# One block of a linear layer by a level of Strassen's algorithm, and a weight load in two halves

## The chip, the cores and the metric

The kernel runs on one core of one Trainium2 chip. The time is the device time of one execution in microseconds (us). Three runs of the kernel before gave 1405.92 to 1406.15 us, with a median of 1406.15 us. Besides these there is one execution under the hardware profiler. Everything said of single instructions comes from that one.

## The reference

`x` is 1024 x 512, `weight` holds 64 matrices of 512 x 512, and everything is fp32.

```python
out_lin = x @ lin_w.T + lin_b
xv = jnp.einsum('bf,efm->bem', x, weight)
zp = jnp.einsum('bf,efm->bem', jnp.square(x), jnp.square(weight))
interaction = 0.5 * jnp.sum(jnp.square(xv) - zp, axis=1)
return out_lin + interaction
```

There are 64 large products, `x @ weight[e]`, whose squares are summed, one product of squares, and one small product for the linear layer, `x @ lin_w.T`. The change is in the linear layer.

## The kernel before

**The blocks.** `x` is cut into four blocks by rows r and by columns kk: A11 (0, 0), A12 (0, 1), A21 (1, 0) and A22 (1, 1). Each block has four quarters of 256 columns on 128 partitions. In the names of the code, block "1" is A11, "2" is A12 and "4" is A22, and `xs[:, SLOT[i], SLOT[o]]`, reached as `xsl(i, o)`, is quarter or sum o of block or sum i. The host has laid out `x` and `lin_w.T` so that a block's quarters are contiguous.

**Strassen's algorithm in this kernel.** The main loop multiplies with two nested levels of Strassen's algorithm (its Winograd form): seven products instead of eight, in return for sums of the operands and of the results. `outer_x` makes the sums "5", "6", "7" and "3" of whole blocks (L154 to L176), `inner_x` the four sums of quarters within one block (L178 to L185), and `outer_t` and `inner_t` the sums of the weights. One product of the inner level is called "1", "5", "6", "2", "7", "3" or "4", and these are made in this order. They go to three PSUM banks x, v and y: "1" and "2" to x, "5" and "3" to v, and "6", "7" and "4" to y, which starts as a copy of x after "1". Between two products into the same bank another engine has to read that bank, so TensorE waits for that engine before the second.

**The linear layer before.** It comes ahead of the main loop, while the first weights are being loaded. `lin_w.T` has four row groups k, loaded in `load_lw` (L135), 0 and 1 by ScalarE's queue and 2 and 3 together by SyncE's.

- Rows r = 0: `lin(kk)` (L204 to L222) multiplies A11 (kk = 0) and A12 (kk = 1) directly: eight matmuls of 128x512 each. `lin_out` (L224) then writes twice the sum to `acc[0]` with ScalarE.
- Rows r = 1: `lin_p` (L260) multiplies A21 and A22 by one level of Strassen's algorithm, four matmuls of 128x256 for each of the seven products. `twice` (ScalarE) and `lin_join` (L307, VectorE) write the results to `acc[1]`. The operands' sums are made by `lin_t` (L282, GpSimd) from `lin_w.T`, and by `a21_a22_sums` (L240) from `x`, on VectorE except for the last, which GpSimd makes.

**What sets the order.** There is no scheduler. `Stream` (L14) sorts the pieces by a number t that is written by hand (`st.at(t, fn)`), and every engine gets its instructions in that order. Each engine works through its own in order, and waits at an instruction whose semaphores are not there yet. The pieces around the change are those with t below 0: `lin` at -30 and -22, `lin_out` from -20 to -14, the products of r = 1 from -14 to -2, two steps apart, and the sums of `x` in the table at L587: `inner_x("1")` -29, `inner_x("2")` -22, `a21_a22_sums` -20, `outer_x("5") + inner_x("5")` -16, and `outer_x("6") + inner_x("6")` -3.4. GpSimd's share of this stage is `lin_t`, one sum of A22 (L252), and then the sums of the first weights (`inner_t`, L384, and `outer_t`, L373). The main loop's units (`unit`, L413) start at t = 0, with the x bank's first product at L421.

The DMA semaphores of the queues that SyncE and ScalarE issue are given out in turn from eight. A DMA waits until the one eight places ahead of it has landed.

Of the kernel before, what the change touches and what calls it, by code (L numbers as in the profile page):

```python
# [8 lines left out]
F32 = mybir.dt.float32  # L9
AF = mybir.ActivationFunctionType  # L10
ALU = mybir.AluOpType
# [17 lines left out]
def kernel(  # L29
# [77 lines left out]
    def xsl(i, o):  # L107
        return xs[:, SLOT[i], SLOT[o], :]

    st = Stream()  # L110
# [5 lines left out]
    lw_sb = T6.rearrange("p u l m -> p (u l) m")  # L116
    lw_src = lin_wT.rearrange("(p k) m -> p k m", k=NK)
# [7 lines left out]
    def load_x(r, kk, *parts):  # L125
        src = x[:, 2 * r + kk]
        for w in parts:
            if (r, kk) == (1, 0):
                nc.sync.dma_start(A21[:, w], src[:, w])
                continue  # L130
            (i,) = (i for i, rk in BLOCK.items() if rk == (r, kk))
            dst = a21[i] if w == 3 else xs[:, SLOT[i], w]
            nc.sync.dma_start(dst, src[:, w])

    def load_lw(queue, k):  # L135
        queue.dma_start(lw_sb[:, k], lw_src[:, k])

    for k in range(2):
        load_lw(nc.scalar, k)
    load_x(0, 0, 0, 3, slice(1, 3))  # L140
    load_lw(nc.sync, slice(2, 4))
    load_x(0, 1, slice(0, 3), 3)
# [3 lines left out]
    def quarter(r, kk, n):  # L146

        w = slice(0, 3) if n is None else n
        for i, rk in BLOCK.items():
            if rk == (r, kk):  # L150
                return a21[i] if n == 3 else xs[:, SLOT[i], w, :]
        return A21[:, w, :]

    def outer_x(i, eng=nc.vector):  # L154
        if i in BLOCK:
            return []

        def put(n):
            w = slice(0, 3) if n is None else n

            def of(o):
                return a21[o] if n == 3 else xs[:, SLOT[o], w, :]

            def src(r, kk):
                return quarter(r, kk, n)

            if i == "5":
                eng.tensor_add(of(i), src(1, 0), src(1, 1))
            elif i == "6":
                eng.tensor_sub(of(i), of("5"), src(0, 0))  # L170
            elif i == "7":
                eng.tensor_sub(of(i), src(0, 0), src(1, 0))
            else:
                eng.tensor_sub(of(i), src(0, 1), of("6"))

        return [lambda: put(None), lambda: put(3)]  # L176

    def inner_x(i, eng=nc.vector):  # L178
        add, sub = eng.tensor_add, eng.tensor_sub
        return [  # L180
            lambda: add(xsl(i, "5"), a21[i], xsl(i, "4")),
            lambda: sub(xsl(i, "6"), xsl(i, "5"), xsl(i, "1")),
            lambda: sub(xsl(i, "7"), xsl(i, "1"), a21[i]),
            lambda: sub(xsl(i, "3"), xsl(i, "2"), xsl(i, "6")),
        ]  # L185
# [7 lines left out]
    LIN = {}  # L193
# [7 lines left out]
            ps = psum.tile([P, BK], F32, tag="y", name=f"y_spin{n}", bufs=3)  # L201
            nc.tensor.matmul(ps, zero[:, 0:P], zero, start=True, stop=True)

    def lin(kk):  # L204

        order = [(s, j, l) for s in range(2) for j in range(2) for l in range(2)]
        if kk == 0:
            order.sort(key=lambda o: o[2])
        for s, j, l in order:
            n = 2 * s + j  # L210
            if kk == 0 and l == 0:
# [4 lines left out]
            nc.tensor.matmul(  # L216
                LIN[n],
                quarter(0, kk, (0, 1, 3, 2)[2 * s + l])[:, ts(j, P)],
                lw_sb[:, 2 * kk + l, :],
                start=(kk == 0 and l == 0),  # L220
                stop=(kk == 1 and l == 1),
            )  # L222
# [10 lines left out]
    def lin_x(kk, o):  # L233
# [6 lines left out]
    def a21_a22_sums():  # L240
        def put(kk, o, eng):
            def of(o):
                return lin_x(kk, o)

            raw = a21["4"] if kk else A21[:, 3]
            fn, a, b = {
                "5": lambda: (eng.tensor_add, raw, of("4")),
                "6": lambda: (eng.tensor_sub, of("5"), of("1")),
                "7": lambda: (eng.tensor_sub, of("1"), raw),
                "3": lambda: (eng.tensor_sub, of("2"), of("6")),  # L250
            }[o]()
            fn(of(o), a, b)  # L252

        return [
            lambda o=o, kk=kk: put(kk, o, nc.gpsimd if o == "3" and kk else nc.vector)
            for o in "5673"
            for kk in range(2)
        ]

    def lin_p(o, bank, first):  # L260
        def fn():
            if o == "1":
                for n in "xvy":
                    LIN[n] = psum.tile(
                        [P, BK], F32, tag=n, name=f"{n}_lin", bufs=2 if n == "x" else 3
                    )
                s_lin = spool.tile([P, 2, BK], F32, tag="s", name="s_lin")
                LIN["s2"], LIN["s5"] = s_lin[:, 0], s_lin[:, 1]
            for kk in range(2):
                for j in range(2):  # L270
                    nc.tensor.matmul(  # L271
                        LIN[bank][:, ts(j, HM)],
                        lin_x(kk, o)[:, ts(j, P)],
                        lin_rhs(lw_sb[:, ts(kk, 2)], LT[kk], o),
                        start=(first and kk == 0 and j == 0),
                        stop=True,
                        skip_group_check=True,
                    )

        return fn  # L280
# [13 lines left out]
    def lin_rhs(b, t, o):  # L294
        if o in "123":
            l, u = {"1": (0, 0), "2": (1, 0), "3": (1, 1)}[o]
            return b[:, l, ts(u, HM)]
        return t[:, "5764".index(o)]

    def twice(bank, dst):  # L300
        def fn():
            o = by_j(LIN[dst]) if dst in ("s5", "s2") else acc_blk(1, dst)
            nc.scalar.activation(o, by_j(LIN[bank]), AF.Copy, scale=2.0)

        return fn

    def lin_join(bank, s, blk):  # L307
        def fn():
            nc.vector.scalar_tensor_tensor(
                acc_blk(1, blk),  # L310
                by_j(LIN[bank]),
                2.0,
                by_j(LIN[s]),
                ALU.mult,
                ALU.add,
            )

        return fn

    st.at(-40, spin)  # L320
    for kk in range(2):
        st.at(-30 + 8 * kk, lambda kk=kk: lin(kk))
        st.at(-30 + kk, lambda kk=kk: lin_t(LT[kk], lw_sb[:, ts(kk, 2)]))
    for n in range(4):
        st.at(-20 + 2 * n, lambda n=n: lin_out(n))
    for t, fn in (
        (-14, lin_p("1", "x", True)),
        (-13.5, lambda: nc.scalar.copy(LIN["y"], LIN["x"])),
        (-12, lin_p("5", "v", True)),
        (-11.5, twice("v", "s5")),  # L330
        (-10, lin_p("6", "y", False)),
        (-9.5, twice("y", "s2")),
        (-8, lin_p("2", "x", False)),
        (-7.5, twice("x", 0)),
        (-6, lin_p("7", "y", False)),
        (-5.5, lin_join("y", "s5", 3)),
        (-4, lin_p("3", "v", False)),
        (-3.5, lin_join("v", "s2", 1)),
        (-2, lin_p("4", "y", False)),
        (-1.5, twice("y", 2)),  # L340
    ):
        st.at(t, fn)

    bias = const.tile([P, M], F32, tag="bias", name="bias")

# [189 lines left out]
    for q in range(NQ):  # L535
# [29 lines left out]
        for k, n, r, times in (  # L565
# [5 lines left out]
            for j in range(2):  # L571
                t = g0 + 14 * k + 7 * j + 14.6
# [11 lines left out]
        st.at(-100, lambda kk=kk, v=v: load_w(0, kk, v))  # L584


    for sums, t in (  # L587
        (inner_x("1"), -29),
        (inner_x("2"), -22),
        (a21_a22_sums(), -20),  # L590
        (outer_x("5") + inner_x("5"), -16),
        (outer_x("6") + inner_x("6"), -3.4),
    ):
        for n, fn in enumerate(sums):
            st.at(t + 0.1 * n, fn)
# [236 lines left out]
```

## Time and profile before

| what | value |
|---|---|
| median of three runs | 1406.15 us |
| the profiled execution's own time | 1405.72 us |
| its span, from the first to the last instruction | 1403.9 us |
| TensorE busy | 1399.7 us of the span |
| first matmul of the linear layer | at 4.44 us |
| first matmul of the main loop (L421) | at 30.36 us |

The profile's columns are the start in us from the beginning of the span, the duration, the engine, the line and the instruction with its output and inputs. In brackets stands how long the engine was idle before, and what ended that. A 128x512 fp32 matmul leaves two records and a 128x256 one also two, each half as long. TensorE's instructions overlap, so their cost is read from the distance of the starts, not from the durations.

### The profile page before, as it was taken

Reading aid. Unit: us, or ns where it says so; the run is one execution under the profiler, and the core shown is the slowest. Engines: PE = TensorE matmul, PEld = TensorE weight load, DVE = VectorE, ACT = ScalarE, POOL = GpSimd, SP = SyncE. Lnnn points to the kernel's source line nnn. Section 1 sums busy time; section 2 is a strip of 40 time slices with the busy share of each in tenths; the row PEclk is TensorE's granted clock in tenths of the full one; section 3 lists DMA queues with packets and bytes.
Section 4 is the critical chain, followed back from the end, with each engine's and each line's share of the span. In section 5 each row is a group of like instructions: output and inputs, shape, how many; then the busy total and the mean of one; then the engine's idle time right before and its main releaser. Section 6 shows DMA issues by size and latency. Waiting matters only on the chain.

```text
span 1403.9 us, 11169 instructions
## 1 busy us (share of the span) xinstructions
PE 1399.7 (100%) x3340; PEld 634.8 (45%) x3340; DVE 869.0 (62%) x1263; ACT 620.9 (44%) x825; POOL 1257.8 (90%) x816
## 2 busy tenths in 40 slices
PE   9999999999999999999999999999999999999999
PEld 5444444444444444444444444444444444444446
DVE  6665656656566665656656566565656656566565
ACT  3444353453535444353453535444353453435443
POOL 7989899998999989898998989989898998989984
PEclk9999999999999999999999999999999999999999
DMA  5299898999989989898999989889898999989975
GB/s 217 60 225 213 192 203 175 221 187 218 197 180 225 182 206 210 192 207 174 222 187 217 202 178 224 179 206 209 199 202 175 225 185 217 202 181 221 181 166 135
DMA packets 58108, 273.63 MB, mean 195 GB/s; under 512 B 5440, under 2 KB 8000, under 8 KB 41792
## 3 DMA queue, kind: packets, MB, share of 16 engines
q0 software_dynamic: 36432, 198.20, 72.0%
q1 hardware_dynamic: 21328, 74.19, 15.1%
q10 hardware_dynamic: 288, 0.52, 0.1%
q8 instruction: 27, 0.44, 0.1%
q14 instruction: 33, 0.27, 0.1%
HBM read 72.61 MB, written 2.10 MB: 53 GB/s over the span
## 4 chain that ended last, share of the span: by engine, by line
PE 99%; DMA 0%; DVE 0%; issue 0%
PE y L421 41%; PE v L421 27%; PE x L421 27%; PE lin L216 1%; PE y_last L659 1%; PE x_last L659 0%; PE v_last L659 0%; PE y_lin L271 0%; DMA t<-lin_wT 0%; PE v_lin L271 0%; PE x_lin L271 0%; PE end L722 0%; DVE z L732 0%
## 5 line engine op out<-in xcount | busy, mean ns | idle before, releaser
L421 PE MATMUL y<-t,xs 128*128 128x512 f32 x896 | 421.3, 592 | 0.0
L475 ACT COPY y<-x 128x512 f32<-128x512 f32 x224 | 127.7, 570 | 610.9 <-PE x L421 610.8
L467 DVE TENSOR_TENSOR z<-y,s 128x512 f32<-128x512 f32 x192 | 132.6, 691 | 242.9 <-PE y L421 242.9
L421 PEld LDWEIGHTS y<-t,xs 128*128 128x128 f32 x896 | 170.1, 190 | 214.2 <-issue 210.4
L497 ACT ACTIVATE z<-z 128x1024 f32<-128x1024 f32 x256 | 260.2, 1054 | 12.0 <-POOL z L472 9.4
L421 PE MATMUL x<-w,xs 128*128 128x512 f32 x512 | 248.4, 592 | 0.0
L421 PE MATMUL v<-tp,xs 128*128 128x512 f32 x448 | 228.8, 592 | 0.0
L421 PE MATMUL y<-tp,xs 128*128 128x512 f32 x448 | 228.8, 592 | 0.0
L506 POOL DMA_DIRECT2D acc<-z x190 | 212.9, 1151 | 15.1 <-DMA acc<-z 11.0
L391 POOL TENSOR_TENSOR tp<-w 128x1024 f32<-128x1024 f32 x64 | 174.9, 2734 | 23.8 <-PE y L421 22.6
L421 PE MATMUL x<-t,xs 128*128 128x512 f32 x384 | 188.3, 592 | 0.0
L472 POOL TENSOR_TENSOR z<-z,s 128x1024 f32<-128x1024 f32 x64 | 149.6, 2354 | 42.7 <-DVE s L467 42.7
L467 DVE TENSOR_TENSOR z<-v,s 128x512 f32<-128x512 f32 x192 | 132.6, 691 | 72.5 <-PE v L421 71.0
L458 DVE TENSOR_TENSOR z<-y,z 128x512 f32<-128x512 f32 x192 | 132.3, 689 | 57.9 <-PE y L421 57.9
L380 POOL TENSOR_TENSOR t<-w,t 128x1024 f32<-128x1024 f32 x64 | 164.2, 2728 | 0.0
L458 DVE TENSOR_TENSOR z<-x,z 128x512 f32<-128x512 f32 x192 | 132.1, 688 | 36.6 <-PE x L421 35.1
L421 PEld LDWEIGHTS x<-w,xs 128*128 128x128 f32 x512 | 97.3, 190 | 122.0 <-issue 121.0
L391 POOL TENSOR_TENSOR tp<-t 128x1024 f32<-128x1024 f32 x48 | 130.0, 2708 | 19.2 <-PE y L421 19.1
L421 PEld LDWEIGHTS v<-tp,xs 128*128 128x128 f32 x448 | 85.1, 190 | 107.1 <-issue 103.1
L421 PEld LDWEIGHTS y<-tp,xs 128*128 128x128 f32 x448 | 85.1, 190 | 106.7 <-issue 106.7
L421 PE MATMUL v<-w,xs 128*128 128x512 f32 x256 | 130.7, 592 | 0.0
L446 DVE TENSOR_TENSOR s<-v,z 128x512 f32<-128x512 f32 x160 | 110.5, 691 | 29.4 <-PE v L421 28.7
(114 smaller groups left out, 1475.7 us busy)
## 6 DMA issues: line engine op xcount, KB each, us to landing
w<-weight SPq DMA_DIRECT2D x64, 1024.0 KB, 13.4
acc<-z POOLq DMA_DIRECT2D x128, 512.0 KB, 8.2
w_sum<-w_sb POOLq DMA_DIRECT2D x63, 1024.0 KB, 9.3
acc<-z POOLq DMA_DIRECT2D x62, 1024.0 KB, 8.1
w<-x SPq DMA_DIRECT2D x2, 1024.0 KB, 8.0
out<-z SPq DMA_DIRECT2D x7, 256.0 KB, 2.3
xs<-x SPq DMA_DIRECT2D x2, 384.0 KB, 7.0
t<-lin_wT ACTq DMA_DIRECT2D x2, 256.0 KB, 4.0
```

Of the source, the lines that this page charges most:

```text
L216: nc.tensor.matmul(LIN[n], quarter(0, kk, (0, 1, 3, 2)[2 * s + l])[:, ts(j, P)], lw_sb[:, 2 * kk + l, :], start=(kk == 0 and l == 0), stop ...
L380: nc.gpsimd.tensor_sub(OUTER[i][:, u], a[:, u], b[:, u])
L391: nc.gpsimd.tensor_sub(t, b[:, 1], b[:, :, 0])
L421: nc.tensor.matmul(d[bank], xsl(i, o)[:, ts(j, P)], operand_b(q, i, o), start=start, stop=True, skip_group_check=True,)
L446: nc.vector.tensor_add(o, d[bank], zblk(q, addend, j, b))
L458: nc.vector.tensor_add(zblk(q, dst, j, b), d[bank], zblk(q, addend, j, b))
L467: nc.vector.tensor_add(s if both else zblk(q, dst, j, b), d[bank], s)
L472: nc.gpsimd.tensor_add(place(q, n)[:, 1, j], place(q, src)[:, 1, j], d["s"])
L475: st.at(t0 + 0.5, lambda: nc.scalar.copy(d["y"], d["x"]))
L497: lambda u=u: nc.scalar.activation(z[:, u, j], z[:, u, j], AF.Square),
L506: nc.gpsimd.dma_start(o, z, accum_op=ALU.add)
L659: nc.tensor.matmul(ps[:, ts(j, HM)], last_x(i)[:, (0, 1, 3, 2)[2 * s + l], ts(j, P)], last_w(i)[:, l, :], start=(start and j == 0 and l == 0),
```

## The change

A12's part of the rows r = 0 is no longer multiplied directly. `lin` keeps A11's eight matmuls; the first two of them are cut into two column halves each, in the order (half 0, j 0), (half 0, j 1), (half 1, j 0), (half 1, j 1), and the load of row group 0 of `lin_w.T` is cut in the same halves. `lin_out` writes A11's part to `acc[0]`, and the seven products of A12 follow through `lin_p` with r = 0, two matmuls of 128x256 each, one step of t apart. Their results are added to `acc[0]` by a new `lin_add` on VectorE, which also takes the place of `lin_join` for r = 1:

```diff
-    for k in range(2):
-        load_lw(nc.scalar, k)
+    for u in range(2):
+        load_lw(nc.scalar, 0, ts(u, HM))
+    load_lw(nc.scalar, 1)
...
-    def lin(kk):
-
-        order = [(s, j, l) for s in range(2) for j in range(2) for l in range(2)]
-        if kk == 0:
-            order.sort(key=lambda o: o[2])
+    def lin():
+
+
+        order = [
+            (s, j, l, slice(0, M)) for l in range(2) for s in range(2) for j in range(2)
+        ]
+        order[0:2] = [(0, j, 0, ts(u, HM)) for u in range(2) for j in range(2)]
...
-    def lin_p(o, bank, first):
+    def lin_p(r, o, bank, first):
...
+            kks = range(2) if r else (1,)
+            for kk in kks:
                 for j in range(2):
                     nc.tensor.matmul(
-                        LIN[bank][:, ts(j, HM)],
-                        lin_x(kk, o)[:, ts(j, P)],
+                        LIN[r, bank][:, ts(j, HM)],
+                        lin_x(kk, o, r)[:, ts(j, P)],
                         lin_rhs(lw_sb[:, ts(kk, 2)], LT[kk], o),
...
+    def lin_add(r, bank, addend, dst):
...
+            nc.vector.scalar_tensor_tensor(
+                of(dst), by_j(LIN[r, bank]), 2.0, of(addend), ALU.mult, ALU.add
             )
...
+    for r, t0, dt in ((0, -21.5, 1), (1, -14, 2)):
...
+                ("1", "x", True, copy_y),
+                ("5", "v", True, twice("v", "s5") if r else lin_add(0, "v", 3, "s5")),
+                ("6", "y", False, twice("y", "s2") if r else lin_add(0, "y", 1, "s2")),
+                ("2", "x", False, twice("x", 0) if r else lin_add(0, "x", 0, 0)),
+                ("7", "y", False, lin_add(r, "y", "s5", 3)),
+                ("3", "v", False, lin_add(r, "v", "s2", 1)),
+                ("4", "y", False, twice("y", 2) if r else lin_add(0, "y", 2, 2)),
...
+            st.at(t0 + dt * n, lin_p(r, o, bank, first))
+            st.at(t0 + dt * n + 0.25 * dt, fn)
...
-        (a21_a22_sums(), -20),
-        (outer_x("5") + inner_x("5"), -16),
-        (outer_x("6") + inner_x("6"), -3.4),
+        (a21_a22_sums(), -21, -19.5, -18.5, -16.5, -15.5, -15),
+        (outer_x("5") + outer_x("6"), -14.5),
+        (inner_x("6") + inner_x("5"), -3.4),
```

The last hunk moves VectorE's sums. The sums of A21 and A22 are dealt out between the additions of r = 0. `outer_x("6")` moves ahead of the products of r = 1, beside `outer_x("5")`, and `inner_x("5")` moves behind them.

On VectorE the order of the built kernel, after `inner_x("2")`, is this ("add" is `lin_add` with the product that it follows, z and xs are A21's and A22's sums): z5, add "5", xs5, add "6", z6, add "2", add "7", xs6, add "3", z7, add "4", xs7, z3, the two instructions of `outer_x("5")`, the two of `outer_x("6")`, then for r = 1 add "7" and add "3", then `inner_x("6")` and `inner_x("5")`, and then the main loop. GpSimd's order is unchanged: six instructions of `lin_t`, A22's sum "3", which waits for xs6, and then the weights' sums.

More of the change, by code (lines that the diff above doesn't have):

```diff
@@ L133, in load_x, with load_lw @@
             nc.sync.dma_start(dst, src[:, w])
-    def load_lw(queue, k):
-        queue.dma_start(lw_sb[:, k], lw_src[:, k])
-    for k in range(2):
-        load_lw(nc.scalar, k)
+    def load_lw(queue, k, cols=slice(0, M)):
+        queue.dma_start(lw_sb[:, k, cols], lw_src[:, k, cols])
+    for u in range(2):
+        load_lw(nc.scalar, 0, ts(u, HM))
+    load_lw(nc.scalar, 1)
     load_x(0, 0, 0, 3, slice(1, 3))
@@ L202, in spin @@
             nc.tensor.matmul(ps, zero[:, 0:P], zero, start=True, stop=True)
-    def lin(kk):
-        order = [(s, j, l) for s in range(2) for j in range(2) for l in range(2)]
-        if kk == 0:
-            order.sort(key=lambda o: o[2])
-        for s, j, l in order:
+    def lin():
[3 more added lines that the diff above has]
+        order[0:2] = [(0, j, 0, ts(u, HM)) for u in range(2) for j in range(2)]
+        for s, j, l, cols in order:
             n = 2 * s + j
-            if kk == 0 and l == 0:
+            if n not in LIN:
                 tag = "xxvy"[n]
@@ L216, in lin @@
             nc.tensor.matmul(
[L217 to L221, printed above, removed]
+                LIN[n][:, cols],
+                quarter(0, 0, (0, 1, 3, 2)[2 * s + l])[:, ts(j, P)],
+                lw_sb[:, l, cols],
+                start=(l == 0 and cols.start == 0),
+                stop=(l == 1),
+                skip_group_check=True,
             )
@@ L231, in lin_out, with lin_x @@
         )
-    def lin_x(kk, o):
+    def lin_x(kk, o, r=1):
+        if r == 0:
+            return xsl("2", o)
         if kk == 1:
@@ L263, in fn @@
                 for n in "xvy":
-                    LIN[n] = psum.tile(
-                        [P, BK], F32, tag=n, name=f"{n}_lin", bufs=2 if n == "x" else 3
-                    )
-                s_lin = spool.tile([P, 2, BK], F32, tag="s", name="s_lin")
-                LIN["s2"], LIN["s5"] = s_lin[:, 0], s_lin[:, 1]
-            for kk in range(2):
+                    LIN[r, n] = psum.tile(
+                        [P, BK], F32, tag=n, name=f"{n}_lin{r}", bufs=2 if n == "x" else 3
+                    )
+                s_lin = spool.tile([P, 2, BK], F32, tag="s", name=f"s_lin{r}")
+                LIN[r, "s2"], LIN[r, "s5"] = s_lin[:, 0], s_lin[:, 1]
+            kks = range(2) if r else (1,)
+            for kk in kks:
                 for j in range(2):
                     nc.tensor.matmul(
-                        LIN[bank][:, ts(j, HM)],
-                        lin_x(kk, o)[:, ts(j, P)],
+                        LIN[r, bank][:, ts(j, HM)],
+                        lin_x(kk, o, r)[:, ts(j, P)],
                         lin_rhs(lw_sb[:, ts(kk, 2)], LT[kk], o),
-                        start=(first and kk == 0 and j == 0),
+                        start=(first and kk == kks[0] and j == 0),
                         stop=True,
@@ L301, in fn, with of @@
         def fn():
-            o = by_j(LIN[dst]) if dst in ("s5", "s2") else acc_blk(1, dst)
-            nc.scalar.activation(o, by_j(LIN[bank]), AF.Copy, scale=2.0)
-        return fn
-    def lin_join(bank, s, blk):
+            o = acc_blk(1, dst) if isinstance(dst, int) else by_j(LIN[1, dst])
+            nc.scalar.activation(o, by_j(LIN[1, bank]), AF.Copy, scale=2.0)
+        return fn
+    def lin_add(r, bank, addend, dst):
+        def of(n):
+            return acc_blk(r, n) if isinstance(n, int) else by_j(LIN[r, n])
         def fn():
             nc.vector.scalar_tensor_tensor(
[L310 to L315, printed above, removed]
+                of(dst), by_j(LIN[r, bank]), 2.0, of(addend), ALU.mult, ALU.add
             )
@@ L320, with copy_y @@
     st.at(-40, spin)
+    st.at(-30, lin)
     for kk in range(2):
-        st.at(-30 + 8 * kk, lambda kk=kk: lin(kk))
         st.at(-30 + kk, lambda kk=kk: lin_t(LT[kk], lw_sb[:, ts(kk, 2)]))
     for n in range(4):
[L325 to L342, printed above, removed]
+        st.at(-29 + 0.1 * n, lambda n=n: lin_out(n))
+    for r, t0, dt in ((0, -21.5, 1), (1, -14, 2)):
+        def copy_y(r=r):
+            nc.scalar.copy(LIN[r, "y"], LIN[r, "x"])
+        for n, (o, bank, first, fn) in enumerate(
+            (
+                ("1", "x", True, copy_y),
[5 more added lines that the diff above has]
+                ("4", "y", False, twice("y", 2) if r else lin_add(0, "y", 2, 2)),
+            )
+        ):
+            st.at(t0 + dt * n, lin_p(r, o, bank, first))
+            st.at(t0 + dt * n + 0.25 * dt, fn)
     bias = const.tile([P, M], F32, tag="bias", name="bias")
@@ L584 @@
         st.at(-100, lambda kk=kk, v=v: load_w(0, kk, v))
-    for sums, t in (
+    for sums, *times in (
         (inner_x("1"), -29),
         (inner_x("2"), -22),
-        (a21_a22_sums(), -20),
-        (outer_x("5") + inner_x("5"), -16),
-        (outer_x("6") + inner_x("6"), -3.4),
+        (a21_a22_sums(), -21, -19.5, -18.5, -16.5, -15.5, -15),
+        (outer_x("5") + outer_x("6"), -14.5),
+        (inner_x("6") + inner_x("5"), -3.4),
     ):
         for n, fn in enumerate(sums):
-            st.at(t + 0.1 * n, fn)
+            k = min(n, len(times) - 1)
+            st.at(times[k] + 0.1 * (n - k), fn)
     for i, t in (("7", -4.7), ("3", 36.9)):
```

## The prediction

> **What bounds the kernel now.** I read the page's first part and the chain of waits first.
>
> ```profile
> PE 1399.7 (100%) x3340; PEld 634.8 (45%) x3340; DVE 869.0 (62%) x1263; ACT 620.9 (44%) x825; POOL 1257.8 (90%) x816
> ...
> PE 99%; DMA 0%; DVE 0%; issue 0%
> ```
>
> TensorE (PE) is busy throughout and is 99% of the chain. So a matmul taken away is worth its whole slot, and a wait put ahead of TensorE costs its whole length, since no later idle time can absorb it. Next, the timeline of VectorE (DVE) and GpSimd (POOL) in the linear layer, because the change moves work there:
>
> ```profile
> 14.00 0.41 DVE L252 TENSOR_TENSOR z<-z 128x256 f32<-128x256 f32 x1
> 14.16 2.72 POOL L252 TENSOR_TENSOR xs<-xs 128x256 f32<-128x256 f32 x1 [2.37 <-DVE xs L252]
> ...
> 16.32 0.83 DVE L181 TENSOR_TENSOR xs<-z,xs 128x256 f32<-128x256 f32 x1
> 16.84 2.54 POOL L391 TENSOR_TENSOR tp<-w 128x1024 f32<-128x1024 f32 x1
> 17.19 2.47 DVE L182 TENSOR_TENSOR xs<-xs 128x256 f32<-128x256 f32 x1
> 19.45 1.33 POOL L393 TENSOR_TENSOR t<-w,tp 128x512 f32<-128x512 f32 x1
> 19.58 1.48 DVE L183 TENSOR_TENSOR xs<-xs,z 128x256 f32<-128x256 f32 x1
> 20.86 1.33 POOL L395 TENSOR_TENSOR t<-w,t 128x512 f32<-128x512 f32 x1
> 20.99 1.49 DVE L184 TENSOR_TENSOR xs<-xs 128x256 f32<-128x256 f32 x1
> 22.15 4.85 POOL L380 TENSOR_TENSOR t<-w,w 128x1024 f32<-128x1024 f32 x2
> 26.96 2.35 POOL L391 TENSOR_TENSOR tp<-w 128x1024 f32<-128x1024 f32 x1
> 27.19 0.69 DVE L309 SCALAR_TENSOR_TENSOR acc<-y_lin,s_lin 128x512 f32<-128x512 f32 x1 [4.72 <-PE y_lin L271]
> 28.84 0.69 DVE L309 SCALAR_TENSOR_TENSOR acc<-v_lin,s_lin 128x512 f32<-128x512 f32 x1 [0.96 <-PE v_lin L271]
> 29.40 1.26 POOL L393 TENSOR_TENSOR t<-w,tp 128x512 f32<-128x512 f32 x1
> 29.44 2.03 DVE L170 TENSOR_TENSOR xs<-xs 128x768 f32<-128x768 f32 x1
> ```
>
> The same 256-wide VectorE sum takes 0.41 us at 14.00 and 2.47 at 17.19. At 17.19 it ends at 19.66, 0.28 after GpSimd's instruction (16.84 + 2.54 = 19.38); the next two end 0.28 and 0.29 after theirs. The 768-wide one (29.44) ends 0.81 after. Each VectorE sum thus passes only at the end of one GpSimd instruction, and GpSimd's next begins before VectorE's second. Additions that read PSUM (L309, 0.69) pass unhindered. VectorE was idle for 4.72 us before 27.19, so none of this reached TensorE.
>
> [...]
>
> **Matmuls.** Starts give the slots: the 32 records of the direct products end their slots at 18.27 (first x_lin start), and the 56 records of r = 1 take 30.36 - 18.27 = 12.09, or 0.216 a record, 0.43 for a 128x256 matmul. A 128x512 one is 0.86 (main loop, 30.36 to 31.22). Removed: A12's 8 x 0.86 = 6.87. Added: 14 x 0.43 = 6.04. The two matmuls cut into four halves cost nothing (4 x 0.43). Gain **0.83**, all on the path.
>
> **Loads.** TensorE starts at 4.44 on the first 256 KB of lin_w.T, issued at 0.74 and landed after 3.7; 128 KB of x, issued beside it, took 3.4. A half should land between these; gain 0 to 0.3, I take 0.2 (effective start 4.35 instead of 4.54; the first matmul's record is long). The second half is issued 0.45 later and is needed 0.86 later, so it is in time. Row group 1 is issued a third, at 1.64 instead of 1.19: it lands near 5.9 instead of 5.5, wanted by TensorE at 7.8, and GpSimd's `lin_t` starts about 0.35 later. On SyncE's queue one more DMA shifts the eight semaphores by one: A12's last quarter now waits for the first half (issue 3.06 to about 4.2), and A21, A22, the first weights and the bias queue behind it, each 0.2 to 0.3 later. Before, A12 was complete at 9.8, A21 at 11.0 and A22 at 12.4; the uses below are at 10.6, 13.0 and 14.0. Cost nothing here.
>
> **The products of A12.** After the eight matmuls of A11 TensorE is at 4.35 + 6.87 = 11.22. Each product now has 0.86 where r = 1 has 1.73. The bank's reader takes 0.2 to start, 0.57 (ScalarE copy) or 0.69 (VectorE), and 0.22 until TensorE goes on (in the main loop the copy ends at 31.99 and "6" is effectively at 32.21).
> - "1" 11.22, "5" 12.08. Its sum xs5 of A12, before ready at 11.20, now about 11.55. In time.
> - "6": the copy of x is done at 12.08 + 0.77, so 13.07 instead of 12.94: 0.13. "2" 13.93.
> - "7" waits for add "6". VectorE has z5 (13.02), add "5" (13.36) and xs5 (13.97) ahead, add "6" is 14.31 to 15.00, so "7" is at 15.22 instead of 14.79: 0.43.
> - "3" 16.08. "4" waits for add "7" (16.32 to 17.01): 17.23 instead of 16.94: 0.29. It ends at 18.09.
>
> Waits 0.85, gain 0.83 + 0.19: r = 1 starts at **18.09** instead of 18.27. ScalarE's `lin_out` ends at 12.0, before the first add; its copies of r = 1 lie in the longer products.
>
> **VectorE's sums.** Here I expect the loss. xs6 is dispatched at 16.93 and frees GpSimd's sum of A22 at 17.42, 3.3 later than before (14.16). At that moment VectorE turns to additions from PSUM, so GpSimd gets in at once and then runs its weights' sums without a pause. Behind it VectorE still has z7, xs7, z3, two instructions of `outer_x("5")` and two of `outer_x("6")`, seven sums from SBUF (before: four, L181 to L184), and **behind these add "7" of r = 1, for which product "4" of r = 1 waits**. One GpSimd instruction each, at the durations above (one that follows a 768-wide sum 0.5 to 0.6 longer, as L395 at 30.74, 1.86 against 1.33):
> - A22's sum to 18.14, z7 18.42; L391 to 20.64, xs7 20.93; L393 to 22.04, z3 22.33;
> - L395 to 23.45, `outer_x("5")` 24.26; L380 to 26.44, its second 26.73;
> - L380 to 28.9, `outer_x("6")` 29.71; L391 to 31.9, its second 32.19.
>
> Then add "7" is 32.1 to 32.8 and "4" starts at 33.02. Without a wait it is at 18.09 + 6 x 1.725 = 28.44. A stall of **4.6**. The main loop starts at 33.02 + 1.73 = 34.75 instead of 30.36: **+4.4**.
>
> **The eight inner sums behind.** Add "3" and then `inner_x("6")` and `inner_x("5")` follow, eight sums (before: two of `outer_x("6")` and four), ahead of the first join, L467, for which the first unit's "4" waits. Before, that join ran at 37.35, with "4" barely held (0.04). If the first sum slips in between L393 and L395, seven more GpSimd instructions follow (L395 and six of L172 to L184), the join ends near 41.7, and "4", due at 34.75 + 7.85 = 42.60, doesn't wait. If it loses, one L380 (2.4) more, the join ends near 44.2 and "4" waits 1.8. The dispatches are 0.05 apart, closer than I can place them: 0 to 1.8, I take 0.9. Sum 4.4 + 0.9 = **+5.3**.
>
> GpSimd itself is late by 1.3 to 3 us, TensorE by more; its rows from 38.66 on were 6 us and more ahead of their users (unit "6" needs at 51.99 what was done at 43.3). Nothing later moves but by the same shift. The profiled execution would be 1405.72 + 5.3 = 1411.0; the median of the runs is 0.43 higher, 1411.4.
>
> **Rivals.**
> - **A, not slower:** [...] At 14.16 GpSimd's sum took 2.72 because VectorE's unbroken run went first. If the seven sums run so, at 0.34 or 0.87 each, about 4.2, they end by 23. It decides at 27.5: if `outer_x("6")` is done by then, "4" never waits, and what is left is 0.19: 1406.0. Against it: all sixteen VectorE sums that met a running GpSimd row between 6 and 38 us passed singly, and GpSimd gets in during add "3".
> - **B, one or two fewer pairings:** GpSimd later or VectorE earlier by one 2.4 us instruction leaves a stall of 2.1: +1.9, 1408.1.
> - **C, the clock:** [...] 1413 to 1415.
> - **D, the change doesn't do what it says:** the built order has 14 matmuls of 128x256 where 8 of 128x512 were, so no.
>
> **How the numbers follow.** Forecast 0.55 (own range +3.0 to +7.2, 1409.2 to 1413.4), A 0.20, B 0.13, C 0.12. About 0.2% (2.8 us) can be told from no change: forecast, C and a little of B are slower, 0.70; A and most of B are within it, 0.28; faster 0.02, since matmuls and load together can give 1.1. The range reaches down to A and up to the own range's end, 1405.6 to 1413.6; outside are most of C and the lower tail of A.
>
> **What would show it.** Right: in the profile after, VectorE's rows of `outer_x` end 0.29 or 0.81 after GpSimd rows, its add "7" of r = 1 starts near 32, TensorE's idle time has one wait of 4 to 5 us for VectorE before the last y_lin product, and L421 first starts near 34.75. r = 1 starting near 18.1 shows the first part right. Wrong: L421 first at 30.2, or `outer_x("6")` ended before 27.5.

## The result, and the profile after

Six runs of the changed kernel took 1413.73 to 1414.97 us, with a median of 1414.5 us; six of the kernel before, beside them, had a median of 1406.16 us. The ratio is 1.0059, with a 95% interval of 1.0047 to 1.007: slower by 8.3 us, which is above the upper end of the predicted range. The profiled execution took 1414.7 us, with a span of 1412.9 us (before 1405.72 and 1403.9).

The page's first part and the chain of waits, after. Before, TensorE was 99% of the chain:

```profile
PE 1403.2 (99%) x3356; PEld 639.4 (45%) x3356; DVE 880.6 (62%) x1269; ACT 621.7 (44%) x826; POOL 1256.9 (89%) x816
...
PE 94%; DVE 2%; POOL 2%; DMA 1%; issue 1%; POOLq 0%; ACTq 0%; SPq 0%; DVEq 0%; ACT 0%
```

TensorE is still busy 99% of the span, but the chain now goes through VectorE, GpSimd and the loads for 5% of it. TensorE's waits say where. Behind the colon stand the us in total, how often it waited, and the longest wait:

```profile
PE y_lin L278 <- DVE acc L321: 4.3, 1, 4.3
PE y_lin L278 <- DVE s_lin L321: 1.0, 1, 1.0
...
PE v_lin L278 <- DVE xs L182: 0.4, 1, 0.4
```

Three new waits, all in the linear layer, all for VectorE. The timeline of VectorE and GpSimd after, from the start of VectorE's sums to the additions that end r = 1:

```profile
8.13 0.43 DVE L182 TENSOR_TENSOR xs<-z,xs 128x256 f32<-128x256 f32 x1 [8.13 <-DMA xs<-x]
8.44 1.26 POOL L291 TENSOR_TENSOR z<-t 128x512 f32<-128x512 f32 x1 [8.00 <-DMA z<-x]
...
19.38 0.73 POOL L258 TENSOR_TENSOR xs<-xs 128x256 f32<-128x256 f32 x1 [4.81 <-DVE xs L258]
20.07 2.54 POOL L399 TENSOR_TENSOR tp<-w 128x1024 f32<-128x1024 f32 x1
20.91 1.97 DVE L258 TENSOR_TENSOR xs<-xs,z 128x256 f32<-128x256 f32 x1
...
25.38 5.56 POOL L388 TENSOR_TENSOR t<-w,w 128x1024 f32<-128x1024 f32 x2
26.16 2.58 DVE L169 TENSOR_TENSOR z<-z 128x256 f32<-128x256 f32 x1
28.66 3.10 DVE L171 TENSOR_TENSOR xs<-xs 128x768 f32<-128x768 f32 x1
30.91 3.05 POOL L399 TENSOR_TENSOR tp<-w 128x1024 f32<-128x1024 f32 x1
31.68 2.55 DVE L171 TENSOR_TENSOR z<-z 128x256 f32<-128x256 f32 x1
34.16 0.68 DVE L321 SCALAR_TENSOR_TENSOR acc<-y_lin,s_lin 128x512 f32<-128x512 f32 x1
34.76 0.68 DVE L321 SCALAR_TENSOR_TENSOR acc<-v_lin,s_lin 128x512 f32<-128x512 f32 x1
35.36 0.41 DVE L182 TENSOR_TENSOR xs<-z,xs 128x256 f32<-128x256 f32 x1
```

Two things are to be seen. From 20.07 on each VectorE sum ends just behind one GpSimd instruction: 22.88 (20.91 + 1.97) is 0.27 behind 22.61, and the `outer_x("6")` pair (L171) ends at 31.76, 0.82 behind 30.94, the end of the two L388 instructions that share a row, and at 34.23, 0.27 behind 33.96. And the first sums start at 8.13 and 8.44. Before, they started 2 to 3 us earlier:

```profile
6.27 0.94 DVE L181 TENSOR_TENSOR xs<-z,xs 128x256 f32<-128x256 f32 x1 [6.27 <-DMA xs<-x]
5.66 1.26 POOL L284 TENSOR_TENSOR z<-t 128x512 f32<-128x512 f32 x1 [5.21 <-DMA t<-lin_wT]
```

TensorE's timeline around the stall, after:

```profile
20.06 1.03 PE L278 MATMUL x_lin<-t,z 128*128 128x256 f32 x4
...
34.89 2.07 PE L278 MATMUL y_lin<-z,z 128*128 128x256 f32 x4 [4.31 <-DVE acc L321]
36.76 1.91 PE L278 MATMUL y_lin<-z,xs 128*128 128x256 f32 x4
38.47 1.65 PE L429 MATMUL x<-w,xs 128*128 128x512 f32 x2
39.95 1.02 PE L429 MATMUL v<-tp,xs 128*128 128x512 f32 x2
```

Product "4" takes 38.47 - 34.89 = 3.58 us instead of 1.73, and the main loop's first product 1.48 instead of 0.86. The busy times of the same stretch, cut into windows of 3 us, say why. The last three numbers of a row are PEclk (the clock that TensorE is granted, as a share of full speed), the DMA engines' busy share and their GB/s:

```profile
30.00:33.00 3.00, 0.58 (x3) 0.18 (x1) 3.00 (x2) 0.00 (x0) 3.00 (x2) 0.98 0.00 0
33.00:36.00 3.00, 1.11 (x3) 0.93 (x4) 2.96 (x5) 0.00 (x0) 2.84 (x3) 0.50 0.00 0
36.00:39.00 3.00, 3.00 (x8) 2.24 (x7) 3.00 (x2) 0.29 (x1) 3.00 (x3) 0.50 0.00 0
39.00:42.00 3.00, 3.00 (x7) 1.20 (x6) 2.97 (x5) 1.46 (x3) 2.84 (x4) 0.88 0.00 0
```

The clock was at half from shortly before 33 us to shortly before 40. The last line of TensorE's timeline is the main loop's second product. Before, it stood here:

```profile
31.22 1.02 PE L421 MATMUL v<-tp,xs 128*128 128x512 f32 x2
```

So this is the profile's sum at that product, 39.95 instead of 31.22, against the sum that was predicted:

| term | predicted | measured, and how |
|---|---|---|
| start of r = 1 | -0.18 | +1.79 (20.06 - 18.27) |
| wait of its product "4" | +4.58 | +4.48 (34.89 - 20.06 - 6 x 1.725) |
| clock behind that wait | 0 (rival C) | +2.47 (3.58 - 1.73 + 1.48 - 0.86) |
| first unit's "4" behind the inner sums | +0.9 | 0 (the join waits for TensorE at 44.58) |
| sum | +5.3 | +8.74 |

The shift is still 8.7 us at 1381 us. So all of the loss but some 0.3 us (the spans differ by 9.0) arises in the first 40 us.

### The profile page after: what moved, and what is told of

It is laid out like the page before. It is cut to its first block, busy times and chain, and to the rows that moved or that the text cites. A ratio compares the mean times of both kernels' runs of the same rounds, so it can differ in the third digit from the quotient of the medians.

```text
span 1412.9 us, 11213 instructions
## 1 busy us (share of the span) xinstructions
PE 1403.2 (99%) x3356; PEld 639.4 (45%) x3356; DVE 880.6 (62%) x1269; ACT 621.7 (44%) x826; POOL 1256.9 (89%) x816
## 4 chain that ended last, share of the span: by engine, by line
PE 94%; DVE 2%; POOL 2%; DMA 1%; issue 1%; POOLq 0%; ACTq 0%; SPq 0%; DVEq 0%; ACT 0%
PE y L429 40%; PE x L429 27%; PE v L429 27%; DMA acc<-z 1%; DMA xs<-x 0%; PE y_lin L278 0%; POOL z L480 0%; POOL acc L514 0%; POOL w_sb L658 0%; DVE z L171 0%; DVE z L169 0%; POOL w L638 0%; POOL tp L399 0%; POOL t L642 0%; DVE xs L258 0%
## 5 line engine op out<-in xcount | busy, mean ns | idle before, releaser
L505 ACT ACTIVATE z<-z 128x1024 f32<-128x1024 f32 x256 | 260.1, 1054 | 11.7 <-POOL z L480 9.2
L514 POOL DMA_DIRECT2D acc<-z x190 | 212.8, 1151 | 14.9 <-DMA acc<-z 10.2
L388 POOL TENSOR_TENSOR t<-w,t 128x1024 f32<-128x1024 f32 x64 | 164.5, 2731 | 0.0
```

The costliest lines, as they stand in the source:

```text
L388: nc.gpsimd.tensor_sub(OUTER[i][:, u], a[:, u], b[:, u])
L505: lambda u=u: nc.scalar.activation(z[:, u, j], z[:, u, j], AF.Square),
L514: nc.gpsimd.dma_start(o, z, accum_op=ALU.add)
```

## The experiments

My theory was three causes that add up: the load in halves makes everything behind it late, VectorE's sums pair with GpSimd's ahead of the addition that "4" needs, and the idle time of TensorE costs its clock. The main rival was that the loss is one thing, the stall, and that the late loads only move it about. The medians of the first four kernels below stand beside a median of 1406.24 us of the kernel before. Each kernel has one trace, of one execution, and that one can be longer than the median.

**The load alone, from both sides.** First the changed kernel with row group 0 loaded whole:

```diff
-    for u in range(2):
-        load_lw(nc.scalar, 0, ts(u, HM))
-    load_lw(nc.scalar, 1)
+    for k in range(2):
+        load_lw(nc.scalar, k)
```

> After, with row group 0 of lin_w.T loaded whole as before (its first two matmuls stay cut in halves). Theory 'the halved load made the inputs late': VectorE's first sum starts near 6.3 us instead of 8.13, the products of r = 1 near 18.2 instead of 20.06, and the time falls by about 1.9 us to 1412.6; the wait of 4 to 5 us for VectorE's add before the last product of r = 1 stays, and with it the half clock. Rival 'the inputs came late by chance or because of the order of the queues': VectorE still starts near 8 us and the time stays at 1414.5 within 0.5.

1412.94 us, ratio 1.0045 (1.0031 to 1.0059). VectorE's first sum is back at 6.40 and GpSimd's at 5.81, r = 1 starts at 18.70, "4" waits the same 4.3 us (at 33.53), and the clock falls again (3.58 us for "4"). The halved load thus costs 20.06 - 18.70 = 1.36 us at r = 1. By the ratios it is 0.0014 x 1406 = 2.0 us of the 8.3, but the intervals of the two ratios overlap, and the two traced spans differ by only 0.8 us (1412.9 and 1412.1): behind the stall the low clock costs 3.1 us here instead of 2.5. So the trace shows that the inputs are on time again without the halves, and the halves' price here is no better known than 0.8 to 2.0 us. More than 6 us stay without it.

Then the halves alone, in the kernel before:

```diff
+            order[0:2] = [(0, j, 0, ts(u, HM)) for u in range(2) for j in range(2)]
...
-    for k in range(2):
-        load_lw(nc.scalar, k)
+    for u in range(2):
+        load_lw(nc.scalar, 0, ts(u, HM))
+    load_lw(nc.scalar, 1)
```

> Before, with only the load of row group 0 of lin_w.T and its first two matmuls cut into column halves. Theory 'the halved load made the inputs late': TensorE starts at about 4.3 instead of 4.44 but VectorE's first sum near 8.1 instead of 6.27; TensorE may then wait for row group 1 (landed near 8.2, wanted near 7.9) and for A12's and A21's sums, so 0.3 to 1.5 us slower than before. Rival 'the load is no cause': first sum at 6.3, time 0 to 0.2 us less than before.

1411.96 us, ratio 1.0038 (1.0025 to 1.005): much more than I expected, and the expectation was wrong in kind. Its timeline of VectorE and GpSimd:

```profile
16.84 0.84 POOL L257 TENSOR_TENSOR xs<-xs 128x256 f32<-128x256 f32 x1 [2.04 <-DVE xs L257]
17.02 0.94 DVE L257 TENSOR_TENSOR xs<-xs,z 128x256 f32<-128x256 f32 x1
17.64 2.52 POOL L396 TENSOR_TENSOR tp<-w 128x1024 f32<-128x1024 f32 x1
17.88 2.56 DVE L257 TENSOR_TENSOR z<-z 128x256 f32<-128x256 f32 x1
...
31.20 1.48 DVE L185 TENSOR_TENSOR xs<-xs 128x256 f32<-128x256 f32 x1
32.60 0.68 DVE L314 SCALAR_TENSOR_TENSOR acc<-y_lin,s_lin 128x512 f32<-128x512 f32 x1
```

In the kernel before, GpSimd's sum of A22 at 14.16 took 2.72 us, while five of VectorE's sums went through beside it (14.34 to 16.32). Here, 2.7 us later, it takes 0.84 and goes into the middle of that run. Seven sums from SBUF then pair with GpSimd's weights' sums, the addition is at 32.60 instead of 27.19, and "4" of r = 1 waits 3.9 us, without any of Strassen's new products. So the loads and the pairing are not independent: a load that is 2 us late can set off the pairing, and the kernel before was clear of it by its timing alone. It doesn't come every time to this extent. The five executions took 1408.61 to 1413.65 us, the trace is of the longest, and the shortest has a mean clock of 1.000 where the others have 0.997 to 0.999.

**The place of the sums.** `outer_x("6")` moved behind the additions of r = 1:

```diff
-        (outer_x("5") + outer_x("6"), -14.5),
-        (inner_x("6") + inner_x("5"), -3.4),
+        (outer_x("5"), -14.5),
+        (outer_x("6") + inner_x("6") + inner_x("5"), -3.4),
```

> After, with only the two sums of outer_x('6') moved back behind the additions of r = 1 (ahead of the eight inner sums). Theory 'each of VectorE's sums costs one GpSimd instruction': the add of '7' of r = 1 is no longer behind them, so the wait of 4.3 us before the last product of r = 1 is gone and the clock stays full there; but ten sums instead of eight stand before the main loop's first join, which ends near 45, so the first unit's '4' (due near 40) waits 4 to 5 us instead. Total near 1411 to 1415. Rival 'the wait has another cause (product or load)': the wait before the last product of r = 1 stays near 4 us.

1416.74 us, ratio 1.0075 (1.0062 to 1.0087). "4" of r = 1 doesn't wait any more, and the main loop starts at 32.81 instead of 38.47, but TensorE's waits now have this:

```profile
PE y L429 <- DVE z L475: 6.2, 1, 6.2
```

Ten sums are ahead of the first join now, which runs at 46.23; the first unit's "4" starts behind it at 47.06, and the clock is at 0.50 from 47 to 50 us. The stall goes where the queue of sums goes.

**The clock alone.** Five matmuls of zeros, whose result nothing uses, in TensorE's idle time ahead of "4":

```diff
+    def spin_more():
+        zero = nc.const_aps.tensor(0.0, [P, BK], F32)
+        ps = psum.tile([P, BK], F32, tag="x", name="x_spin", bufs=2)
+        for n in range(5):
+            nc.tensor.matmul(ps, zero[:, 0:P], zero, start=True, stop=True)
+
+    st.at(-2.2, spin_more)
```

> After, with five matmuls of zeros (128x512, results unused) between products '3' and '4' of r = 1, that is in TensorE's idle time. Theory 'the idle time let the clock drop to half, and that cost 2.5 us': the clock stays 1.00, product '4' and the first product of the main loop take 1.73 and 0.86 instead of 3.58 and 1.48, and the time falls by 2 to 2.5 us to about 1412.2. Rival 'those matmuls are slow for another reason (operands, port, PSUM)': they stay slow and the time stays at 1414.5.

1412.65 us, ratio 1.0045 (1.0032 to 1.0057). TensorE's timeline of this kernel:

```profile
30.90 4.47 PE L331 MATMUL x_spin<-const-float32-0.0 128*128 128x512 f32 x10
35.38 1.13 PE L278 MATMUL y_lin<-z,z 128*128 128x256 f32 x4
36.35 1.03 PE L278 MATMUL y_lin<-z,xs 128*128 128x256 f32 x4
37.21 1.02 PE L436 MATMUL x<-w,xs 128*128 128x512 f32 x2
38.07 1.02 PE L436 MATMUL v<-tp,xs 128*128 128x512 f32 x2
```

"4" starts 0.49 later than in the changed kernel, and yet the main loop's second product is 1.88 earlier (38.07 against 39.95): "4" takes 1.83 and the first product 0.86. The clock is worth 0.49 + 1.88 = 2.4 us, as the sum above has it. By the ratios it is 0.0014 x 1406 = 2.0, again with overlapping intervals. So the rival "one stall" doesn't hold as it was put. The late load and the low clock can each be taken away while the stall stays, and each was worth something of its own. The clock hangs on the stall, though: where the stall moved (above), the clock fell behind it there.

**What makes the loads late.** The rows of a half are 1 KB long instead of 2 KB, and there is one DMA more. The kernel before, with row group 0 split by partitions instead, keeps the 2 KB:

```diff
+    for h in range(2):
+        ps = slice(64 * h, 64 * h + 64)
+        nc.scalar.dma_start(lw_sb[ps, 0], lw_src[ps, 0])
+    load_lw(nc.scalar, 1)
```

> Before, with row group 0 of lin_w.T loaded by two DMAs of 64 partitions each, so the rows of 2 KB stay whole and the number and order of the DMAs are those of the change. Theory 'the halved rows (1 KB packets, twice as many) made the later loads late': row group 1 lands near 5.6, VectorE's first sum stays near 6.3 us and the time stays within 0.4 us of before. Rival 'one more DMA ahead (ScalarE's queue, the semaphores shifted by one) made them late': the first sum near 8.2 us and the time near 1412, as with the column halves.

1409.78 us beside 1406.14, ratio 1.0025 (1.0015 to 1.0035). Row group 1 took 7.5 us from issue to landing (before 4.3, from 1.19 to 5.5), GpSimd's first sum starts at 9.64 and VectorE's at 7.50. So it isn't the short rows; the additional DMA is enough. The time is below the 1412 expected for this, and it isn't the same loss. TensorE needs both halves here and starts at 5.63 instead of 4.44, its first two matmuls take 3.45 us (5.63 to 9.08) instead of 1.82, and "4" of r = 1 waits 1.9 us behind paired sums, at full clock. Where the additional DMA stands was tried last (under "The half on another queue").

**An order that doesn't pair.** If GpSimd gets A22's last sum only when VectorE is through, nothing should pair. In the changed kernel with the whole load:

```diff
-        (a21_a22_sums(), -21, -19.5, -18.5, -16.5, -15.5, -15),
+        (a21_a22_sums(), -21, -19.5, -18.5, -14.05, -15.5, -15, -14.9, -14.04),
...
-        (inner_x("6") + inner_x("5"), -3.4),
+        (inner_x("6"), 10.6),
+        (inner_x("5", nc.gpsimd), 43.35),
```

> After with the whole load, A22's sum xs6, which frees GpSimd, put behind outer_x('5') and outer_x('6') on VectorE, inner_x('6') moved behind the first unit's joins and inner_x('5') to GpSimd. The same products and additions as after. Theory 'each of VectorE's SBUF sums costs one GpSimd instruction': those sums now run before GpSimd starts, at 0.41 and 0.94 us each; no wait of 4 us before the last product of r = 1, no half clock, no wait at the first unit's '4'. The time falls from 1412.9 to 1405.8 to 1406.8. Rival 'the wait has another cause (product order, PSUM bank)': it stays at 4 us and the time above 1411.

1410.79 us, ratio 1.0031 (1.002 to 1.0043). In the linear layer it does what it should: VectorE's four `outer_x` instructions take 0.42 or 0.95, no product of r = 1 waits for VectorE, and the main loop starts at 30.78. This is the sum that took 3.10 us at 28.66 in the changed kernel:

```profile
21.22 0.95 DVE L170 TENSOR_TENSOR xs<-xs 128x768 f32<-128x768 f32 x1
```

So the stall was the pairing's doing, although the time is 4 us above what I expected. TensorE now waits 2.9 us ahead of 80.27. In the trace, which is of the shortest of six executions, the clock is kept; four of the others have a mean of 0.999. VectorE's timeline there:

```profile
73.17 0.69 DVE L453 TENSOR_TENSOR s<-v,z 128x512 f32<-128x512 f32 x1
78.93 0.69 DVE L474 TENSOR_TENSOR z<-v,s 128x512 f32<-128x512 f32 x1 [5.07 <-POOL xs L183]
```

The join at 78.93 writes a buffer that one of GpSimd's four `inner_x("5")` sums still reads, and GpSimd comes to these only at 76.70. Then products "3", "7" and "4" of r = 0 were put in another order as well, so that none waits for an addition, and the first two matmuls were made whole again (not among these lines):

```diff
+            t = t0 + dt * n
+            if r == 0:
+                t = {"7": -16.5, "3": -17.5, "4": -13}.get(o, t)
...
+        (a21_a22_sums(), -21, -20.9, -20.8, -15.5, -20.7, -20, -18, -15.4),
+        (outer_x("5") + outer_x("6"), -15.9),
```

> As e6_pool_later, and the products of r = 0 in the order 1, 5, 6, 2, 3, 7, then '1' of r = 1, then '4' of r = 0, with A21's and A22's sums in VectorE's idle time, and the first two matmuls whole again. Theory: the two waits for VectorE's adds in r = 0 (0.4 and 0.3 us, 0.85 with the copy) shrink to the copy's 0.13, so the saved 0.83 us of matmuls shows: 0.3 to 0.8 us less than before, 1405.4 to 1405.9. Rival 'the products of 0.86 us leave waits in any order': 1406.2 or more.

1408.4 us, ratio 1.0015 (1.0009 to 1.0022), again more than expected. The main loop starts at 29.78, 0.58 ahead of the kernel before. This is lost again at 78.05 and behind it, with waits of 1.6 us behind the same join and 0.7 us behind ScalarE. Then `inner_x("6")` was put into VectorE's idle time of 6.3 us behind r = 1, and `inner_x("5")` behind the first joins on VectorE:

```diff
-        (inner_x("6"), 10.6),
-        (inner_x("5", nc.gpsimd), 43.35),
+        (inner_x("6"), -3.4),
+        (inner_x("5"), 10.6),
```

> The kernel of c1_order with the four inner sums of row group 6 in VectorE's idle time of 6.3 us ahead of the first join, and the four of row group 5 behind it, on VectorE too, so that GpSimd has none of them. My theory (what c1_order lost after 60 us was GpSimd's 2.9 us of four inner sums, which put its sums of 88 us 1.8 us late): no wait after 60 us, GpSimd's rows at 86 to 88 us back near those of the kernel before, and the 0.58 us won up to the main loop's first product stays: 1405.4 to 1405.8 us. Rival (the four sums of row group 6 now stand beside GpSimd's rows of 26 to 35 us, pair with them one by one and hold up the first join at 35.3 us until a bank is short): a wait of 0.5 to 1.5 us for that join near 37 to 39 us, 1406.2 to 1407.2.

1406.82 us (1405.43 to 1407.75) beside 1406.49: ratio 1.0003 (0.9995 to 1.0012). It can't be told from the kernel before. The expected gain of 0.6 us doesn't show in the median. The profiled execution was the shortest of the 13, with a span of 1403.6 us against 1403.9; it has no wait behind the linear layer, and the four sums pair with GpSimd (2.43, 2.45, 1.48, 1.48) at no cost, since the join they hold ends at 37.20 and is needed later. No version here is measurably faster than the kernel before.

**The half on another queue.** The last kernel with the halves put back, first both on ScalarE's queue as in the change, then with the second half on SyncE's, which is this edit:

```diff
+        order[0:2] = [(0, j, 0, ts(u, HM)) for u in range(2) for j in range(2)]
...
-    for k in range(2):
-        load_lw(nc.scalar, k)
+    load_lw(nc.scalar, 0, ts(0, HM))
+    load_lw(nc.scalar, 1)
...
-    load_x(0, 0, 0, 3, slice(1, 3))
+    load_x(0, 0, 0)
+    load_lw(nc.sync, 0, ts(1, HM))
+    load_x(0, 0, 3, slice(1, 3))
```

> c2_inner_on_dve with the first row group of lin_w.T loaded, and the first two matmuls run, in halves of the columns as in the changed kernel. If the halves cost by the loads behind them alone (row group 1 and the next part of x land some 2 us later, as in the changed kernel and in the kernel before with two row halves): TensorE waits 0.3 to 2 us in the linear layer's first products and stays that late, 1406.0 to 1407.8 us, without any wait behind VectorE's sums. Rival (the delay is lost in slack once the order of the sums doesn't hang on it): within 0.3 us of c2_inner_on_dve.

> c3_halved with the second half issued on SyncE's queue, behind the first part of x, instead of on ScalarE's ahead of row group 1. If it is ScalarE's queue that is late through one more DMA of its own: row group 1 lands near 5.5 us again, as in the kernel before, and only the parts of x behind the half come later by up to 0.5 us. Rival (one more DMA in the first microseconds slows all that is then in flight, whatever the queue): the rate of 3.5 to 6 us is below 250 GB/s again and row group 1 lands at 7.5 us or later. Times by either: within 1 us of c3_halved, below it in the first case.

With both on ScalarE's queue the median is 1409.31 us, ratio 1.0019 (1.0012 to 1.0027), which is above both expected ranges. With one on SyncE's it is 1407.07 us, ratio 1.0004 (0.9996 to 1.0012), 2.2 us lower, where 1 was expected at most. The DMA issues of the two, KB and us from issue to landing, first both on ScalarE's queue:

```profile
xs<-x SPq DMA_DIRECT2D x1, 256.0 KB, 6.7
t<-lin_wT ACTq DMA_DIRECT2D x1, 256.0 KB, 6.8
```

and one on SyncE's:

```profile
t<-lin_wT ACTq DMA_DIRECT2D x1, 256.0 KB, 3.6
xs<-x SPq DMA_DIRECT2D x1, 256.0 KB, 5.6
```

Row group 1 lands after 3.6 us when it is the second DMA of its queue, and after 6.8 when it is the third, with the same halves. The main loop starts at 30.14 and 32.29, where it starts at 29.78 with the load whole. So the halves with one on SyncE's queue cost 0.4 us here, and with the third DMA on ScalarE's queue 2.1 more. In these traces the half does bring a small gain, but it is lost behind it: with one half on SyncE's queue A11's products end at 11.34 instead of 11.56, and A12's then take 5.85 us up to "1" of r = 1 (17.19) instead of 5.27, with one wait of 0.3 us for an addition. Both kernels also wait 1.2 us for ScalarE near 85 us. ScalarE's row in the last kernel:

```profile
80.98 2.00 ACT L527 ACTIVATE w_sb<-w 128x1024 f32<-128x1024 f32 x2 [3.59 <-DMA w_sum<-w_sb]
```

It waits for a transfer that GpSimd issued at 69.19 and that took 11.7 us. In the kernel before, GpSimd issued it at 65.63, it took 10.2 us, and ScalarE had it in time at 77.56. GpSimd is later in all kernels of this order, since it was made to start its weights' sums later. That this also makes the spread of the version before these two (1405.43 to 1407.75) is likely but not shown, since only its shortest run has a trace.

## Why the prediction was right or wrong

The direction, the place and the main mechanism were right; the forecast of +5.3 us was 3 us short. Two steps failed: the loads, at "Cost nothing here", and the clock's fall, which was given a chance instead of a place in the sum.

- **What bounds the kernel: right.** Every wait put ahead of TensorE was paid in full: the 8.7 us at 40 us are still there at 1381 us.
- **Matmuls, 0.83: right as far as it shows.** In the version whose products of r = 0 wait for no addition, the main loop starts 0.58 us earlier than before. That is 0.83, less 0.08 of waiting for a copy, and less 0.16 because A11's products end at 11.56 instead of 11.40 (18.27 - 6.87).
- **Loads: this step failed.** It said that row group 1 lands near 5.9, the later parts 0.2 to 0.3 later, and "Cost nothing here". Row group 1 landed at 8.24 and A11's last part at 8.03. The wrong part was to take the landing as the issue plus an unchanged flight. The issue was near enough (A12's last quarter went out at 3.71, after 0.7 us of waiting for the first half), but the flights (the last number, in us) were not, here before and then after:

```profile
t<-lin_wT ACTq DMA_DIRECT2D x1, 256.0 KB, 4.3
xs<-x SPq DMA_DIRECT2D x1, 256.0 KB, 4.5
...
t<-lin_wT ACTq DMA_DIRECT2D x1, 256.0 KB, 6.6
xs<-x SPq DMA_DIRECT2D x1, 256.0 KB, 6.4
```

- **Products of A12: the step was sound, its input was not.** With the whole load the waits between "1" (12.06) and r = 1 (18.70) are 6.64 - 6.04 = 0.60, where I had 0.85. In the changed kernel they are 20.06 - 11.85 - 6.04 = 2.17, through the late sums: 1.3 us more than predicted.
- **What the step left out: TensorE's rate at the start.** A11's products ended at 11.85 instead of 11.22, because the first two 128x512 matmuls took 2.36 us (4.32 to 6.68) where I had 1.72. The windows show the full clock there, but they count as full what the trace has no clock record for, and its first record begins at 5.59 us. Up to there the records of the 128x256 matmuls start 0.43 us apart (4.32, 4.75, 5.18, 5.60), and then 0.22. In the kernel before, the first record begins at 3.64, ahead of the first matmul, and the first two take 1.82 us (4.44 to 6.26). With the whole load they take 2.24 (4.67 to 6.91), and with the row halves 3.45. So TensorE began at half rate here, and how long that lasted differed from trace to trace, with the halved load and without. Together with the waits this makes the 1.97 us by which r = 1 started later than predicted.
- **VectorE's sums: right.** Seven instructions, one GpSimd instruction each: they ended 0.27 to 0.29 us behind theirs, the 768-wide ones 0.82. The wait is 4.48 us against 4.58, at the product named. Rival A (the sums run through ahead of GpSimd's) is out. An addition from PSUM took the same 0.68 us beside a running GpSimd instruction (20.31, 34.16) as beside none (16.38). What makes the two engines alternate was not shown.
- **The eight inner sums: 0 instead of 0.9.** The first slipped in (35.36, 0.41 us), which was one of the two cases.
- **The clock: this step failed too, and rival C was no rival.** I gave the clock's fall 0.12, and set its price beside the forecast (1413 to 1415 us against 1411.4) instead of in it. That it would seldom come was my own estimate, which no trace had shown. It came with the stall and cost 2.47 us, which the five matmuls of zeros gave back. In the profiles with a wait of 3.9 to 6.2 us (this kernel, with the whole load, the halves in the kernel before, `outer_x("6")` behind) the clock fell each time, and in all six runs of this kernel the mean granted clock is 0.997 to 0.999. In this kernel the clock fell at 32.89, 2.3 us after TensorE had stopped (30.58). Waits of 1.9 us (row halves in the kernel before) and of 2.9 us (ahead of 80.27, above) left the clock alone. What length of wait it takes was not shown.

The errors are -0.9 (inner sums), +1.3 (waits through late loads), +0.6 (rate at the start), +2.5 (clock) and -0.1 (stall): 3.4 us on the profile's sum, 3.1 on the medians. That the stall's size fits so well is in part luck: r = 1 and GpSimd's release were both late by 2.0 us (20.06 instead of 18.09, 19.38 instead of 17.42), so their distance stayed. In the kernel before with column halves, a delay in the loads changed the pairing itself.

## What to carry to other kernels

A forecast stall on TensorE as long as those here (3.9 to 6.2 us) should have the clock's price in its own sum (here 2.4 to 3.1 us). A harmless order of VectorE's and GpSimd's sums may rest on the moment at which GpSimd is released: before a load is touched, look at what 2 us of delay would do to that order. A DMA set ahead of others in a queue can cost more than its issue time: here, with both halves on ScalarE's queue, the issue took 0.45 us and the main loop started 2.5 us later. Another queue can be the better place: with one half on SyncE's it started 0.4 us later.

## What was not expected of the hardware

- One more DMA of 128 KB ahead on ScalarE's queue went with 6.6 to 7.5 us from issue to landing for the next one, in all six kernels that had it, with rows of 1 KB and of 2 KB. The six others took 3.6 to 4.6 us. The 256 KB of SyncE's queue that were issued at the same time came late with it (5.8 to 7.1 us instead of 4.5 in the kernel before), but they came late without it too: 5.6 us with the half on SyncE's queue, and 6.6 us in the kernel "An order that doesn't pair", which loads row group 0 whole. So the lateness of `x` has a further cause that wasn't tested. In the changed kernel all DMA engines together moved 145 GB/s from 4 to 5 us, where the kernel before moved 365. What in the queue does this stays open.
- GpSimd's 256-wide sum took 2.72 us in the kernel before, where VectorE's unbroken run went on beside it, and 0.72 to 0.84 in seven of the other kernels, where it was released at 16.84 to 22.93 instead of 14.16: beside additions from PSUM, in the middle of the run or behind it. Which engine went first was not the same in both.
- The low clock outlasted the wait. In the changed kernel's trace it was at half from 32.89 to 39.72, for 6.83 us, and TensorE was back at 34.89. In the kernel before with column halves it fell near 32.1, 2.7 us after TensorE had stopped (the mean granted clock of 30 to 33 us is 0.85, and 0.50 behind that). At half the clock, half of the time from TensorE's return to the full clock is an estimate of the loss. The full clock of the first row is read from the trace's clock records; the others are estimates from the mean clock of 3 us windows and, with the whole load, from the distances of the matmuls:

| kernel | TensorE stops | TensorE is back | full clock | half of the rest |
|---|---|---|---|---|
| changed | 30.58 | 34.89 | 39.72 | 2.4 |
| with the whole load | 29.22 | 33.53 | 39.7 | 3.1 |
| before, in column halves | 29.43 | 33.33 | 38.9 | 2.8 |
| `outer_x("6")` behind | 40.83 | 47.06 | 52.8 | 2.9 |

The clock fell in these four waits, of 3.9 to 6.2 us, and stayed in those of 1.9 and 2.9 us. What decides it was not shown; no run tested it by itself.
